# Sharing the sixteen transfers of a band between SyncE and GpSimd in another way

## The chip, the cores and the metric

The kernel runs on one core of one Trainium2 chip. The metric is the device time in microseconds of one execution; the time of a kernel is the median of its runs.

## What is computed

The input x holds 32 images of 256 channels and 32 x 32 pixels. Two layers follow each other, each with a group norm of its input (32 groups of 8 channels) in front and the input added behind:

```python
x = x + conv3x3(groupnorm(x))        # inputs and product rounded to 10 bits of mantissa, plus bias
x = x + involution7x7(groupnorm(x))
# the involution, n = groupnorm(x):
y = relu(batchnorm(w1 @ n))                     # 64 channels
w = (w2 @ y + b2).reshape(16 groups, 49 taps, 32, 32)
out[g, c] = sum over taps of w[g, tap] * patch of n[g, c] at tap      # 16 channels a group
```

So in the second layer every pixel has its own 7 x 7 filter for each of 16 groups, computed from the pixel itself.

## The kernel before

**Work and stages.** All 32 images pass through one pipeline that is written out by hand: a loop over slots `n` (line 537), sixteen to an image. In each slot it emits whatever is due in it. `front(b)` (line 275) is a generator that is advanced up to twice a slot and does the first layer of an image that comes later, up to the normed input `xn`, its reduced form `y_sb` and the transposed `pixels`. `sums(b, m)` (line 480) and `add_windows` (line 511) do the involution on PE and add its result to x.

**Bands.** The involution's sum over taps runs on PE as a product of pixels and of a band: for a piece of 8 rows of an image (`k`, four to an image, 128 in all) an SBUF tile of 128 pixels by 2 sides, in which the filters of each pixel stand at the place where they act. Three such tiles (`NBAND`, line 62) take turns. The filters have to be brought from one layout to another, and that is done through a scratch tensor `wd` in HBM:

- `weights(b, r0)` (line 390): PE computes the filters of four rows, DVE adds the bias and writes them to the ring `w_sb` (line 416).
- `scatter(b, k)` (line 454): seven transfers of 160 KB, from `w_sb` to `wd`, one for each column of the filter, all issued by SyncE (line 465).
- `load_bands(b, k)` (line 467): sixteen transfers (`JC`) of 70.2 KB, from `wd` to the band, each to eight partitions and two sides. With `SHARE = 8` SyncE (`nc.sync`) issues those with `i` 7 and 15, GpSimd (`nc.gpsimd`, the POOL of the profile) the other fourteen (lines 477 and 478).
- `sums(b, m)` reads the band on PE (line 503), two calls for each band; its first matmul waits for all sixteen transfers.

**Order around the change.** SyncE's queue carries everything else that moves: the loads of x (line 105, two of 512 KB for each image), the scatters, its two band transfers, and the stores of the result (line 524). GpSimd's queue carries, after its memsets at the start, band transfers alone. Each queue works in the order of the program. The scatter of band `k` of image `b` is emitted in slots 16b-13, 16b-9, 16b-5 and 16b-3 for k = 0 to 3, its loads in slot 16b+4k-9, its first sums in slot 16b+4k. Thus SyncE's band transfers stand behind the scatter of the next band in slots in which both are due, and ahead of those that follow. Completion is told by eight semaphores for SyncE's transfers and eight for GpSimd's, which are used in turn: a transfer isn't issued before the one eight earlier in its queue has landed. The first GpSimd transfer of a band also waits for the band's scatters and for PE's last use of the tile, and the first scatter that overwrites a part of `wd` waits for the loads that read it an image before.

Of the kernel before, what the change touches and what calls it, by code (L numbers as in the profile page):

```python
# [14 lines left out]
B, C, H, W = 32, 256, 32, 32  # L15
# [44 lines left out]
ROW = S * WPIX  # L60
WR = 4
NBAND = 3
SHARE = 8
NPIX = 6
RING = 24
FRONT = -56
# [5 lines left out]
def tile_quant_conv_then_involution(  # L72
# [16 lines left out]
    nc = tc.nc  # L89
# [377 lines left out]
    def load_bands(b, k):  # L467

        band = bands[(b * K + k) % NBAND]
        for i in range(JC):  # L470
            j = i // 2 + i % 2 * JC // 2
            src = bass.AP(
                tensor=wd.tensor,
                offset=wd.offset + k * TR * ROW + (j + PAD1) * WPIX,
                ap=[[ROW - 1, TR], [JC * WPIX, SIDES], [1, WPIX]],
            )
            queue = nc.sync if i % SHARE == SHARE - 1 else nc.gpsimd
            queue.dma_start(band[j::JC, :, j * WB : j * WB + WPIX], src)  # L478

    def windows(b, m):  # L480
# [49 lines left out]
    def due(n, lag):  # L530

        b, i = divmod(n - lag, per)
        return (b, i) if 0 <= b < B else (None, None)

    with tc.manual_schedule():
        fronts = {}
        for n in range(FRONT, B * per + 2):
            b, i = due(n, FRONT)
# [10 lines left out]
            b, i = due(n, 0)  # L549
            if b is not None and i % 2 == 0:  # L550
                sums(b, i // 2)
            b, i = due(n, 1)
# [6 lines left out]
            b, i = due(n, 2)  # L559
            if b is not None and i == 2 * (M - 1 - SIDES):  # L560
                store(b, 0)
            b, i = due(n, -LEAD)
# [3 lines left out]
            b, i = due(n, -LEAD + 1)  # L566
# [4 lines left out]
            b, i = due(n, LOAD)  # L571
# [3 lines left out]
            b, i = due(n, 3 - 4 * NBAND)  # L575
            if b is not None and i % 4 == 0:
                load_bands(b, i // 4)
# [37 lines left out]
```

## Time and profile before

| | us |
|---|---|
| median of three runs | 1411.43 |
| lowest and highest | 1402.78, 1411.64 |
| the profiled execution, its time | 1416.45 |
| its span, from the first to the last instruction | 1414.7 |
| GpSimd's first band transfer issued at | 77.3 |
| GpSimd's last band transfer issued at | 1401.3 |

The profile is of one execution. PE is TensorE's matmuls, PEld its loads of weights, DVE VectorE, ACT ScalarE, POOL GpSimd and SP SyncE, whose work is only to issue. In a line such as `POOL band L478 <- DMA band<-wd: 171.5, 223, 2.9` the engine and line that waited stand on the left, what ended the wait on the right, then the sum in us, the number of times and the longest. Where a page says `issue`, the profile shows nothing that was waited for. The granted TensorE clock is 0.978 of full speed over the span. By lines, the chain of work that ended last gives 24% of the span to band transfers, 19% to the convolution's matmuls, 15% to the involution's sums, 9% to the filters' matmuls, 7% to scatters and 5% to POOL's issuing of band transfers.

### The profile page before, as it was taken

What the parts mean: (1) busy time and instruction counts of PE and PEld (TensorE: products, weight loads), DVE (VectorE), ACT (ScalarE), POOL (GpSimd) and SP (SyncE); (2) the same over time, 40 slices, a digit from 0 to 9 for tenths busy, and PEclk for the clock granted to TensorE, in tenths of its full rate; (3) what the DMA queues carried; (4) which work ended last, traced back from release to release, by engine and by line L of the source; (5) the groups of instructions that cost most, each with busy time, mean ns of one, the idle gap of its engine ahead of it and who ended that gap; (6) DMA issues with size and microseconds to landing.
All of it is one profiled execution on the core that took longest, in us unless ns stands there. A gap on an engine that the chain in (4) does not pass through costs nothing.

```text
span 1414.7 us, 70076 instructions
## 1 busy us (share of the span) xinstructions
PE 1265.2 (89%) x29440; PEld 802.2 (57%) x29440; DVE 933.0 (66%) x3180; ACT 729.8 (52%) x1699; POOL 1003.5 (71%) x1817
## 2 busy tenths in 40 slices
PE   4899899999999899989999999999999999999665
PEld 1456565566565566655566556565566556655543
DVE  4567667767677677766767667767667676766642
ACT  5775555455555445555545555554556454553300
POOL 7067767686776777767777777677776767777774
PEclk9999999999999999999999999999999999999976
DMA  6099899999999999999999999999999999999995
GB/s 212 6 228 283 251 277 276 281 262 285 277 273 264 287 268 269 294 260 270 289 267 287 268 277 253 273 280 273 274 289 271 268 279 282 278 270 262 258 258 165
DMA packets 366232, 369.33 MB, mean 261 GB/s; under 512 B 78624, under 2 KB 308192, under 8 KB 365664
## 3 DMA queue, kind: packets, MB, share of 16 engines
q1 hardware_dynamic: 279904, 235.72, 57.2%
q0 software_dynamic: 86016, 129.14, 34.5%
q8 instruction: 234, 3.83, 1.2%
q14 instruction: 78, 0.64, 0.1%
HBM read 183.81 MB, written 180.74 MB: 258 GB/s over the span
## 4 chain that ended last, share of the span: by engine, by line
PE 47%; DMA 31%; issue 7%; POOL 5%; DVE 4%; ACT 3%; SPq 2%; POOLq 0%; DVEq 0%; ACTq 0%
DMA band<-wd 24%; PE pc L320 19%; PE acc L503 15%; PE pw L398 9%; DMA wd<-w_sb 7%; POOL band L478 5%; PE py L368 3%; DVE w_sb L416 2%; PE pt L383 2%; SPq L465 2%; ACT junk L210 1%; DVE x L519 0%; DVE w_sb L147 0%; ACT xn L269 0%; DVE q L334 0%
## 5 line engine op out<-in xcount | busy, mean ns | idle before, releaser
L478 POOL DMA_DIRECT2D band<-wd x1792 | 978.0, 548 | 397.8 <-DMA band<-wd 249.0
L416 DVE TENSOR_TENSOR w_sb<-pw,b_sb 128x16 f32<-128x16 f32 (+9 forms) x1920 | 454.0, 350 | 386.9 <-PE pw L398 363.2
L320 PE MATMUL pc<-xq,wq 128*128 128x496 f16 (+3 forms) x2304 | 536.5, 379 | 31.3 <-ACT xq L269 21.4
L503 PE MATMUL acc<-band,pixels 64*32 64x190 f32 (+1 forms) x16384 | 420.5, 323 | 78.9 <-DMA band<-wd 39.6
L503 PEld LDWEIGHTS acc<-band,pixels 64*32 64x32 f32 x16384 | 298.3, 108 | 171.1 <-issue 101.5
L320 PEld LDWEIGHTS <-wq 128*128 128x128 f16 x2304 | 206.4, 98 | 328.9 <-issue 114.6
L398 PE MATMUL pw<-w_sb,y 64*32 64x224 f32 (+1 forms) x8192 | 296.6, 333 | 31.1 <-issue 29.4
L519 DVE TENSOR_TENSOR x<-acc,x 128x380 f32<-128x380 f32 (+1 forms) x512 | 261.7, 511 | 35.7 <-PE acc L503 26.8
L398 PEld LDWEIGHTS pw<-w_sb,y 64*32 64x32 f32 x8192 | 182.8, 107 | 63.0 <-issue 43.9
L387 ACT COPY pixels<-pt 128x512 f32<-128x512 f32 x128 | 73.6, 575 | 238.2 <-PE pt L383 238.2
L210 ACT ACTIVATE junk<-x 128x512 f16<-128x512 f32 (+1 forms) x192 | 146.5, 763 | 20.7 <-DVE x L336 15.2
L210 ACT ACTIVATE junk<-x,mean 128x1024 f16<-128x1024 f32 x128 | 147.1, 1149 | 4.3
L241 ACT ACTIVATE s<-back,eps 128x2 f32<-128x2 f32 x64 | 18.9, 296 | 193.7 <-DVE back L226 193.6
L334 DVE TENSOR_SCALAR q<-pc 128x512 f16<-128x512 f32 x128 | 87.2, 682 | 16.5 <-PE pc L320 16.3
L269 ACT ACTIVATE xn<-x,off,rstd 128x512 f32<-128x512 f32 x128 | 96.1, 799 | 0.0
L336 DVE SCALAR_TENSOR_TENSOR x<-q,bias_sb,x 128x512 f32<-128x512 f16 x128 | 92.1, 719 | 0.2
L383 PEld LDWEIGHTS pt<-ident,xn 128*128 128x128 f32 x512 | 64.0, 142 | 27.4 <-issue 3.2
L383 PE MATMUL pt<-ident,xn 128*128 128x128 f32 x512 | 78.1, 275 | 0.9 <-ACT pixels L387 0.9
L231 ACT ACTIVATE mean<-back 128x2 f32<-128x2 f32 x64 | 12.7, 199 | 127.6 <-DVE back L226 127.6
L269 ACT ACTIVATE xq<-x,off,rstd 128x1024 f16<-128x1024 f32 x64 | 75.8, 1227 | 0.1
L368 PEld LDWEIGHTS py<-xn,w_sb 128*64 128x64 f32 x2048 | 63.0, 139 | 16.5 <-issue 8.1
L368 PE MATMUL py<-xn,w_sb 128*64 128x64 f32 x2048 | 67.8, 224 | 2.3 <-ACT xn L269 1.8
(40 smaller groups left out, 370.7 us busy)
## 6 DMA issues: line engine op xcount, KB each, us to landing
wd<-w_sb SPq DMA_DIRECT2D x896, 160.0 KB
band<-wd POOLq DMA_DIRECT2D x1792, 70.2 KB
x<-in_x SPq DMA_DIRECT2D x64, 512.0 KB
out<-x SPq DMA_DIRECT2D x64, 512.0 KB
band<-wd SPq DMA_DIRECT2D x256, 70.2 KB
band<-in_w SPq DMA_DIRECT2D x2, 1152.0 KB
w_sb<-in_w SPq DMA_DIRECT2D x2, 196.0 KB
wd<-band SPq DMA_DIRECT2D x2, 180.0 KB
```

Source lines behind the costliest of these rows:

```text
L210: nc.scalar.activation(junk[:, n0:n1], src[:, h, n0:n1], func, bias=bias, accum_out=self.sums[:, i : i + 1])
L269: nc.scalar.activation(dst, src, AF.Identity, bias=self.off[:, one], scale=self.rstd[:, one])
L320: nc.tensor.matmul(pc.rearrange("p (r c) -> p r c", c=W)[:, r0 - nt * RT : r1 - nt * RT, c0:c1], wq[:, kh, k, mh * P : (mh + 1) * P], xq[: ...
L334: nc.vector.tensor_scalar(q, pc, F16_MAX, -F16_MAX, ALU.min, ALU.max)
L336: nc.vector.scalar_tensor_tensor(xt[:, mh, cols], q, bias_sb[:, mh : mh + 1], xt[:, mh, cols], ALU.add, ALU.add)
L368: nc.tensor.matmul(py[i * CR : (i + 1) * CR, cols], w1_sb[:, kh, :], px[:, r : r + 2], start=kh == 0, stop=kh == CH - 1,)
L383: nc.tensor.transpose(pt[:, i, h * P : (h + 1) * P], xn[:, h, (m + i) * P : (m + i + 1) * P], ident)
L398: nc.tensor.matmul(pws[i][t * TW : (t + 1) * TW, r, : dj.stop - dj.start], y_sb[b % 2][half, (r0 // 2 + r) * W : (r0 // 2 + r + 1) * W], w ...
L416: nc.vector.tensor_tensor(to, pws[i][:p, r : r + rows, e, d0 * G : d1 * G].rearrange("p r (d g) -> p r d g", g=G), b2_sb[:p, e, d0 * G : d ...
L478: queue.dma_start(band[j::JC, :, j * WB : j * WB + WPIX], src)
L503: nc.tensor.matmul(at[t * TW : (t + 1) * TW, h, :, f - top : l - top], px[p, a, v * GC : v * GC + TW], of[:, :, 2 * a + v, f - top : l - top],
L519: nc.vector.tensor_tensor(x_at, of, x_at, ALU.add)
```

## The change

SyncE issues the last of the sixteen transfers of a band alone, and GpSimd fifteen. For the four bands of the last image SyncE issues every second one, eight, and GpSimd eight. Over the whole run SyncE has 156 band transfers where it had 256, and GpSimd 1892 where it had 1792. The transfers themselves, their order within a band and all other instructions stay as they are.

```diff
-SHARE = 8
+SHARE = 16
+LAST_SHARE = 2
...
     def load_bands(b, k):

         band = bands[(b * K + k) % NBAND]
+        share = LAST_SHARE if b == B - 1 else SHARE
         for i in range(JC):
             j = i // 2 + i % 2 * JC // 2
...
-            queue = nc.sync if i % SHARE == SHARE - 1 else nc.gpsimd
+            queue = nc.sync if i % share == share - 1 else nc.gpsimd
             queue.dma_start(band[j::JC, :, j * WB : j * WB + WPIX], src)
```

## The prediction

> **What bounds the kernel now.** I read the page first: busy times, then the DMA queues.
>
> ```profile
> PE 1265.2 (89%) x29440; PEld 802.2 (57%) x29440; DVE 933.0 (66%) x3180; ACT 729.8 (52%) x1699; POOL 1003.5 (71%) x1817
> ...
> q1 hardware_dynamic: 279904, 235.72, 57.2%
> q0 software_dynamic: 86016, 129.14, 34.5%
> ```
>
> No engine is full, but the two DMA queues (q1 is SyncE's, q0 is GpSimd's) together hold 91.7% of the sixteen DMA engines over the whole span, start and end included. So next I asked for the steady part in windows, restricted to what touches the bands. The columns are the stretch, its length, busy time and count of PE, PEld, DVE and POOL, the granted clock, the DMA share and GB/s.
>
> ```profile
> 100.00:400.00 300.00, 91.07 (x3648) 65.25 (x3648) 0.00 (x0) 220.63 (x405) 0.99 0.98 274
> 400.00:700.00 300.00, 93.88 (x3712) 66.84 (x3712) 0.00 (x0) 218.62 (x401) 0.99 0.97 275
> 700.00:1000.00 300.00, 90.16 (x3648) 64.26 (x3648) 0.00 (x0) 218.32 (x401) 1.00 0.98 273
> 1000.00:1150.00 150.00, 46.52 (x1856) 32.69 (x1856) 0.00 (x0) 113.46 (x209) 0.99 0.98 277
> ...
> 1210.00:1310.00 100.00, 32.23 (x1311) 22.50 (x1293) 0.00 (x0) 76.46 (x141) 1.00 0.96 272
> ```
>
> POOL's count is the number of band transfers that it issued: 1416 in 1050 us, one in 0.742 us, so a band of fourteen takes 10.38 us. The DMA engines stand at 0.978 there. The last line is a stretch in which nearly all loads of x are over (one pair is left, at 1228 us), and POOL goes at 0.709 us a transfer. Then I asked whom POOL waits for from 300 to 1200 us, and what its line looks like over the whole run (durations are min/median/max in ns):
>
> ```profile
> POOL band L478 <- DMA band<-wd: 171.5, 223, 2.9
> POOL band L478 <- issue: 38.6, 69, 5.9
> POOL band L478 <- DMA wd<-w_sb: 16.4, 27, 2.7
> POOL band L478 <- DMA x<-in_x: 3.8, 2, 3.0
> ```
>
> ```profile
> L478 POOL DMA_DIRECT2D band<-wd x1792: 547/547/683, 77.3 to 1401.3; - x200
> L478 SPq DMA_DIRECT2D band<-wd x256: 569/766/2121, 81.2 to 1388.6; - x128
> ```
>
> An issue takes POOL 547 ns. The rest of the 742 ns is mostly the first wait: each POOL transfer carries a wait for the one eight before it (eight completion semaphores in turn), so POOL has at most eight under way. By the trace's semaphore records the sixteenth increment comes 5.1 us after the issue on average, and eight issues last only 8 x 0.547 = 4.4 us. POOL hardly ever waits for PE to free a band, and little for scatters. So POOL runs without a pause that another engine imposes: it sets the pace, and what slows it is the time that its transfers spend in full DMA engines. PE is next: in the same windows without the restriction it is busy 280 of 300 us, 0.93, so a band can't get below some 9.7 us.
>
> **What the skill says.** "DMA: Bandwidth & Descriptors", section "Issuing engines are not separate DMA queues": transfers from all engines run on the same sixteen DMA engines. The trace agrees, since a transfer's descriptors are the same by both routes (16 of 4496 B, which took 253 ns each on average on both queues, by the packet records). By this the change takes no work from the DMA engines. Section "Why a DMA increments its semaphore by 16 and not by 1": the number of DMA engines for one transfer is the largest factor up to 16 of both outer dimensions; from SyncE the lowest-numbered are taken and the issuer adds the missing counts, from GpSimd consecutive ones from a moving start, and all sixteen count. A band transfer's outer dimension is 8. The trace agrees on the count: 249 of 256 transfers of SyncE show nine updates of their semaphore (eight engines, and one for the missing eight), POOL's show sixteen. Which eight they are, the trace doesn't tell; I take the page's word. Then SyncE's two transfers a band always go to the same eight DMA engines, two descriptors on each.
>
> **The change part by part.**
>
> (a) SyncE issues one transfer fewer for each of 124 bands: about 0.77 us of its queue (the median above). SyncE isn't the pace, so this is worth at most what others wait for scatters: POOL's 16.4 us in 900. I count nothing; the cover is SyncE's own waits for DVE. If the cover weren't there, 124 x 0.77 = 95 us would be at stake, but POOL's wait for scatters limits that to about 20 us.
>
> (b) POOL issues one more for each of these bands, 15 in place of 14. At the present pace it costs 0.742 us, at most 124 x 0.742 = +92 us. But the pace isn't fixed: it follows the load of the DMA engines. From the windows: DMA work per POOL transfer is 0.7415 x 0.9775 = 0.725 us in the steady part, and 0.709 x 0.96 = 0.681 us once the x loads are gone. Work fell by 0.044, the pace by 0.0325: 0.74 of each microsecond of DMA work shows in the time. The part that isn't DMA work is then 0.7415 - 0.74 x 0.725 = 0.21 us a transfer (0.14 to 0.28, since the shares have two digits). One transfer moved with total DMA work unchanged costs this part: +0.21 us a band, +26 us.
>
> (c) The eight DMA engines that SyncE's transfers use get relief. Per band they now have 14 (their part of POOL's) + 4 descriptors, the other eight 14. After the change it is 15 + 2 and 15. The fuller ones lose one descriptor, 0.253 us a band; the emptier ones gain one. POOL's next issue waits for all sixteen counts, so the fuller engines decide. At 0.74 this is worth 0.19 us a band, -23 us. From both sides: nothing if a transfer's slowest engine is as often one of the others, 0.253 us (-31 us) if the eight engines are the bound outright.
>
> (b) and (c) together: 124 x (0.21 - 0.19) = +2.5 us. For (c) I take the value at 0.74 and not zero, because 18 descriptors with the scatters and x come to more work than the others have, in engines that stand at 0.98 on average.
>
> (d) The last image: eight by SyncE and eight by POOL, where it was two and fourteen. Here is SyncE's end before:
>
> ```profile
> 1360.48 5.97 SPq L465 DMA_DIRECT2D wd<-w_sb  x7
> 1366.55 1.25 SPq L478 DMA_DIRECT2D band<-wd  x2
> 1368.17 5.62 SPq L465 DMA_DIRECT2D wd<-w_sb  x7
> 1373.89 1.54 SPq L478 DMA_DIRECT2D band<-wd  x2
> 1375.55 0.40 SPq L524 DMA_DIRECT2D out<-x  x1
> 1376.63 6.66 SPq L465 DMA_DIRECT2D wd<-w_sb  x7
> 1383.39 0.57 SPq L524 DMA_DIRECT2D out<-x  x1
> 1384.07 5.09 SPq L478 DMA_DIRECT2D band<-wd  x4
> ```
>
> POOL is relieved of 24 transfers, about 24 x 0.68 = 16 us (56 took from 1363.9 to 1401.85 us), and would be done long before. SyncE gets 24 more, at 0.57 to 0.77 us: 14 to 18 us. Twelve of them stand ahead of the last band's scatters, and the other twelve are behind everything, so nothing hides them, save some 2 us of SyncE's own waiting. Its last issue moves from 1389.2 to between 1401 and 1408 us; POOL's was at 1401.85. So SyncE takes over as the last, and the end moves by -1 to +6 us: I take +2.
>
> Sum: the profiled execution had a span of 1414.7 us in 1416.45 us. Its span becomes 1414.7 + 2.5 + 2 = 1419. That execution was 5 us over the median of 1411.43, so I forecast 1411.4 + 4.5 = 1416 us.
>
> **Rivals.** *POOL pays and nothing is given back.* The relief of eight engines doesn't show, because the counts of all sixteen come late alike. Then (b) stands alone, with its bounds: 124 x 0.14 to 0.28 = +17 to +35 us, plus the end: 1430 to 1448 us. At its far end, where the pace doesn't follow load at all, +92: 1505 us. For it: the waits of POOL are for its own transfers; POOL has no free time. Against: the pace did follow when the x loads stopped. *The eight engines are the bound outright.* Then a descriptor less is 0.253 us a band, and POOL's own part is hidden: -31 us, 1382 us; it decides as soon as POOL's waiting falls from 0.195 to below 0.144 us a transfer, because then 15 transfers take what 14 took (10.38/15 = 0.692). For it: engines at 0.98 on average with an uneven load; against: POOL's pace rose less than the work fell. PE's 0.93 leaves room for this gain, and for little more. *SyncE as the bound*, relieved by (a): at most 20 us, 1393 us; against it stands that it waits for DVE. *The change doesn't do what it says:* excluded; the program's order has 1892 transfers on POOL's queue and 156 on SyncE's, nothing else moved.
>
> **How the numbers follow.** A difference under 1% (14 us) is about what the measurement of this kernel can't tell from none: its three runs span 1402.8 to 1411.6. The forecast, that the two sides cancel, has 0.43, with its own range 1400 to 1425; POOL pays, 0.30 (of which 0.03 for over 1450); the eight engines or SyncE outright, 0.22, at 1382 to 1397; 0.05 for what I don't see, spread over both sides. That gives faster 0.25, same 0.43, slower 0.32. Leaving out some 0.1 at each end, the range is 1385 to 1450 us.
>
> **What would show it.** In the steady part POOL's count per 300 us should rise from 402 to about 430 (15 in 10.4 us), its mean spacing fall to 0.69 us, with less waiting for its own transfers, and the DMA share stay at 0.97 to 0.98. If POOL pays, the count stays near 415 and the DMA share falls to 0.95 or so. If the eight engines were the bound, the count is above 440. At the end SyncE's last band issue should come after POOL's. I'm wrong if PE begins to wait for bands more than the 12 us in 900 that it does now, or if scatters come late.

## The result, and the profile after

The changed kernel takes 1466.01 us (median of 4 runs, 1459.51 to 1472.25) where the one before took 1408.91 on the same chip (four runs, of which the forecast had three): a ratio of 1.041, with an interval of 1.036 to 1.045. The forecast was 1416 us with a range to 1450, so the time lies outside it, on the slow side. The two profiled executions differ a little less, 1462.67 us (span 1460.9) against 1416.45, because the one of before lay above its median and the one of after below.

The page of the changed kernel, its busy times and DMA queues:

```profile
PE 1264.7 (87%) x29440; PEld 811.0 (56%) x29440; DVE 932.5 (64%) x3180; ACT 729.6 (50%) x1699; POOL 1057.7 (72%) x1917
...
q1 hardware_dynamic: 277504, 228.52, 53.3%
q0 software_dynamic: 90816, 136.35, 35.0%
```

Only POOL works much longer than before, by 54 us: a hundred issues of 0.547 us. (The weight loads, PEld, have 9 us more; PE, VectorE and ScalarE have the same work.) 7.2 MB have gone over from q1 to q0, and the DMA engines are less full, 88.3% where they were 91.7%. The windows of the steady part, restricted to what touches the bands, with a stretch after the last load of x (issued at 1267.7 us):

```profile
100.00:400.00 300.00, 90.26 (x3584) 65.98 (x3584) 0.00 (x0) 226.89 (x417) 0.98 0.94 266
400.00:700.00 300.00, 88.89 (x3520) 64.18 (x3520) 0.00 (x0) 227.89 (x418) 0.99 0.94 266
700.00:1000.00 300.00, 89.63 (x3584) 63.94 (x3584) 0.00 (x0) 229.00 (x420) 0.99 0.93 263
1000.00:1150.00 150.00, 44.51 (x1728) 31.80 (x1728) 0.00 (x0) 107.56 (x198) 0.98 0.94 263
```

```profile
1280.00:1350.00 70.00, 22.36 (x896) 15.66 (x896) 0.00 (x0) 55.81 (x103) 1.00 0.93 261
```

POOL issued 1453 transfers in 1050 us, one in 0.723 us. It was one in 0.742: POOL got faster by 2.6%, where fifteen in place of fourteen needed 7%. So a band takes 15 x 0.723 = 10.84 us in place of 10.38. The DMA share fell to 0.94. These are the marks that the prediction had set for "POOL pays" (about 415 a stretch, 0.95), not for its own forecast (430, 0.97). POOL's waits from 300 to 1200 us, with PE's wait for bands under them (the last line is that of the kernel before), and POOL's and SyncE's lines over the whole run:

```profile
POOL band L480 <- DMA band<-wd: 137.3, 159, 3.4
POOL band L480 <- issue: 36.9, 46, 3.7
POOL band L480 <- DMA wd<-w_sb: 27.2, 33, 3.4
...
PE acc L505 <- DMA band<-wd: 47.0, 33, 3.3
...
PE acc L503 <- DMA band<-wd: 12.1, 8, 3.2
```

```profile
L480 POOL DMA_DIRECT2D band<-wd x1892: 547/547/681, 76.5 to 1443.7; - x190
L480 SPq DMA_DIRECT2D band<-wd x156: 567/602/1872, 80.7 to 1447.1; - x156
```

POOL waits less for its own transfers (137 us, it was 172), and SyncE issues its own faster (median 602 ns, it was 766). The relief is there, but it is small. Who waits now is PE: its wait for bands is 47.0 us where it was 12.1, which the prediction had named as a sign of being wrong. Its other sign, late scatters, shows faintly: POOL waits 27.2 us for them where it waited 16.4. They aren't the loss: in runs below with fifteen and with sixteen transfers on GpSimd that wait is 18.8 and 13.4 us. Of the end, SyncE's timeline:

```profile
1421.48 6.08 SPq L480 DMA_DIRECT2D band<-wd  x8
1427.66 0.40 SPq L526 DMA_DIRECT2D out<-x  x1
1428.41 6.37 SPq L466 DMA_DIRECT2D wd<-w_sb  x7
1434.88 2.44 SPq L526 DMA_DIRECT2D out<-x  x1
1437.42 10.27 SPq L480 DMA_DIRECT2D band<-wd  x16
```

SyncE issues the last band transfer, at 1447.1 us, after POOL's last at 1443.7. From POOL's last issue for the band before the last image to the end of the span it is 50.2 us; before it was 51.3. So the last image costs nothing, and the whole loss lies in the 124 bands before it: 48 us between the profiled executions, counted from POOL's first band transfer, and 57 between the medians, so 0.39 to 0.46 us a band.

### The profile page after: what moved, and what is told of

It reads as the page before. It is cut to its first block, busy times and chain, and to the rows that moved or that the text cites. A ratio compares the mean times of both kernels' runs of the same rounds, so it can differ in the third digit from the quotient of the medians.

```text
span 1460.9 us, 70087 instructions
## 1 busy us (share of the span) xinstructions
PE 1264.7 (87%) x29440; PEld 811.0 (56%) x29440; DVE 932.5 (64%) x3180; ACT 729.6 (50%) x1699; POOL 1057.7 (72%) x1917
## 4 chain that ended last, share of the span: by engine, by line
PE 42%; DMA 32%; DVE 7%; POOL 6%; issue 5%; SPq 5%; ACT 2%; POOLq 0%; DVEq 0%; ACTq 0%
DMA band<-wd 22%; PE pc L321 15%; PE acc L505 15%; DMA wd<-w_sb 9%; PE pw L399 9%; POOL band L480 6%; SPq L466 5%; DVE w_sb L417 4%; PE py L369 2%; PE pt L384 1%; DVE x L521 1%; ACT junk L211 1%; DMA out<-x 1%; DVE w_sb L148 0%; DVE q L335 0%
## 5 line engine op out<-in xcount | busy, mean ns | idle before, releaser
L480 POOL DMA_DIRECT2D band<-wd x1892 | 1032.2, 548 | 386.0 <-DMA band<-wd 221.3
L505 PEld LDWEIGHTS acc<-band,pixels 64*32 64x32 f32 x16384 | 303.2, 108 | 221.4 <-issue 128.1
L399 PE MATMUL pw<-w_sb,y 64*32 64x224 f32 (+1 forms) x8192 | 302.1, 337 | 22.0 <-issue 20.8
L399 PEld LDWEIGHTS pw<-w_sb,y 64*32 64x32 f32 x8192 | 189.4, 108 | 53.6 <-issue 38.6
```

The costliest lines, as they stand in the source:

```text
L399: nc.tensor.matmul(pws[i][t * TW : (t + 1) * TW, r, : dj.stop - dj.start], y_sb[b % 2][half, (r0 // 2 + r) * W : (r0 // 2 + r + 1) * W], w ...
L505: nc.tensor.matmul(at[t * TW : (t + 1) * TW, h, :, f - top : l - top], px[p, a, v * GC : v * GC + TW], of[:, :, 2 * a + v, f - top : l - top],
```

## Experiments

Times are medians, ratios are against the kernel before on the same chip, with a 95% interval; a gain or loss in us is the ratio's. A pace of POOL is always 1050 us, from 100 to 1150, over the band transfers counted there.

**The two halves of the change.** First the steady part alone, then the last image alone:

```diff
-LAST_SHARE = 2
+LAST_SHARE = 16
```

> The change without its last image: SyncE issues one of sixteen in all 128 bands. If GpSimd's fifteenth transfer is the whole loss (0.37 to 0.46 us a band), this is as slow as the changed kernel or a little slower, 1462 to 1475 us, since the last image then has fifteen on GpSimd as well. If the split of the last image were what cost time, this is well below the changed kernel, 1420 us or less.

1461.41 us, 1.041 (1.038 to 1.045): the whole loss.

```diff
-SHARE = 16
+SHARE = 8
 LAST_SHARE = 2
```

> The last image alone is changed: eight and eight there, two and fourteen elsewhere. The changed kernel's end, counted from the last issue of the band before the last image, is 50.2 us and before's 51.4, so the theory that GpSimd's count in the other images is the loss gives the time before, 1405 to 1412 us. The rival, that SyncE's late scatters at the end cost time, gives 1415 us or more.

1405.76 us, 1.002 (1.000 to 1.004): no difference that counts. What is left to explain is fifteen and one in place of fourteen and two.

**One transfer less, on either queue.** From the kernel before, a transfer of each band left out, SyncE's first (shown) or one of GpSimd's (`JC // 2 - 2` in the same place):

```diff
         for i in range(JC):
+            if i == JC // 2 - 1:
+                continue
```

> Leaves work out: of SyncE's two transfers of a band (fourteen stay on GpSimd) the first is not issued at all, so a column of the band keeps its old contents. It is the relief of SyncE and of its eight DMA engines without the transfer on GpSimd. The theory of the prediction (the eight engines decide, 0.74 of 0.253 us a band) gives -24 us or more, 1385 us or less. The theory that GpSimd's own queue sets the pace and hardly follows the DMA load gives at most a third of that, 1400 to 1410 us.

> Leaves work out: of GpSimd's fourteen transfers of a band one is not issued; SyncE keeps its two. The counterpart of the run without one of SyncE's. If a transfer on GpSimd costs three times one on SyncE, this gains 60 to 82 us, or less where PE, busy 0.93 of the time, stops it: 1325 to 1350 us. If both cost alike (data on the DMA engines alone), 24 us, about 1380 us.

Without SyncE's: 1378.09 us, 0.983 (0.979 to 0.987), a gain of 24 us. Without GpSimd's: 1380.64 us, 0.981 (0.976 to 0.986), 26 us. The first is what the prediction's relief had asked for. The second contradicts a simple price list, in which a transfer costs three times as much on GpSimd: at fourteen and two, taking a transfer from either queue is worth about the same. What the two runs share is a sixteenth of the band's data. But they don't end at the same limit. Here is one window without SyncE's transfer, then one without GpSimd's, and of the latter POOL's wait for scatters from 300 to 1200 us:

```profile
400.00:700.00 300.00, 93.84 (x3856) 67.53 (x3840) 0.00 (x0) 228.68 (x420) 1.00 0.96 277
...
400.00:700.00 300.00, 91.59 (x3704) 64.34 (x3688) 0.00 (x0) 210.92 (x386) 0.99 0.98 273
...
POOL band L480 <- DMA wd<-w_sb: 65.7, 30, 7.2
```

Without SyncE's transfer the DMA share falls to 0.96, and GpSimd's fourteen take 1050/1449 x 14 = 10.15 us a band (counts of 408, 420, 414 and 207). Without one of GpSimd's the share stays at 0.98, and POOL's wait for scatters goes from 16.4 to 65.7 us: it is GpSimd that waits there.

**The data, or the place in the queue.** A transfer of 1 KB in place of the real one: once added on GpSimd after the band's transfers (shown), once put where SyncE's was left out.

```diff
+    spare = const.tile([P, 2, 16], F32, name="spare")
+    few = bass.AP(tensor=w1.tensor, offset=w1.offset, ap=[[1000, TR], [64, SIDES], [1, 16]])
...
+        nc.gpsimd.dma_start(spare[:TR], few)
```

> The kernel before, with one more transfer on GpSimd for each band that moves 1 KB (sixteen pieces of 64 B into a spare tile) and nothing else: the issue and the completion semaphore of a fifteenth transfer without its data. From the runs so far a real transfer more on GpSimd costs the 58 us of the change and the 24 us that SyncE's relief gave, 82 us, and 0.6 us of other work there 30 us. If beside the issue the data counts alone, this costs about 30 us, 1430 to 1440 us. If the turn of the eight semaphores counts as well, 50 to 65 us, 1455 to 1468 us.

> Leaves work out: as in the run without SyncE's first transfer, but in its place SyncE issues one of 1 KB to a spare tile, so its queue is as long as before and only the data is gone. If it was the data on the DMA engines that gave 24 us, the gain stays: 15 to 25 us, 1378 to 1390 us. If it was SyncE's time or its semaphores, the gain is lost: 1398 to 1408 us.

On GpSimd the tiny transfer costs 65 us: 1471.52 us, 1.046 (1.039 to 1.053), at least as much as moving a real one there did (58), and a little over the range for the turn of the semaphores. So the loss of the change is not in the data of the fifteenth transfer; it is in its being there. On SyncE, with the data gone and the transfer still issued, 1393.60 us, 0.990 (0.981 to 0.998): 14 of the 24 us stay, within wide bounds. The run lies between the two expected ranges, nearer to the one of the data; how much SyncE's own issue is worth isn't settled by it.

**Other work in GpSimd's time.** The kernel before, with two fills of a small tile after each band's transfers:

```diff
+    spare = const.tile([P, BUSY], F32, name="spare")
...
+        for _ in range(2):
+            nc.gpsimd.memset(spare, 0.0)
```

> The kernel before, and after each band's transfers GpSimd also fills a small spare tile twice, about 0.6 us of its time for each band without any transfer. If GpSimd's own time sets the pace, each band is later by most of it: +50 to +75 us, 1460 to 1485 us. If the eight completion semaphores and the DMA engines set it, the work fits into time in which GpSimd waits anyway: +0 to +25 us, below 1435 us.

1433.22 us, 1.021 (1.018 to 1.024), +30 us. It fell between the two expectations. The fills, by the view of their tile:

```profile
L483 POOL MEMSET spare<- x256: 297/308/322, 85.8 to 1419.6; 128x240 f32 x128
```

0.62 us of POOL's time a band costs 0.23 us a band. A part of GpSimd's time was thus free in the kernel before: it isn't simply full. And the tiny transfer, at the same place and with 0.57 us of POOL's time, cost 0.51 us a band, over twice as much. So a transfer costs more on this queue than other work of the same length; whether that is the turn of the eight semaphores wasn't tried by itself.

**Whether the DMA engines still decide at fifteen.** GpSimd issues the first fifteen, the sixteenth is left out:

```diff
-            queue = nc.sync if i % SHARE == SHARE - 1 else nc.gpsimd
+            if i == JC - 1:
+                continue
+            queue = nc.gpsimd
```

> Leaves work out: GpSimd issues the first fifteen transfers of each band and nobody the sixteenth. It is the change in its other images with a sixteenth of the band's data taken off the DMA engines. At fourteen and two, taking a transfer's data away gave 24 to 26 us from either queue. If at fifteen GpSimd's turn of eight semaphores is the bound and no longer the DMA engines (a floor of 0.72 us a transfer, 10.8 us a band), it stays near the changed kernel: 1448 to 1466 us. If the DMA engines still decide, 1435 to 1443 us.

1467.15 us, 1.040 (1.036 to 1.045): as slow as the changed kernel, with a sixteenth less data. Its windows (counts 412, 417, 419 and 206 in the four stretches, two of them shown) have the pace of 0.722 us of the changed kernel:

```profile
400.00:700.00 300.00, 87.19 (x3524) 63.32 (x3526) 0.00 (x0) 227.74 (x417) 0.97 0.93 258
700.00:1000.00 300.00, 89.15 (x3568) 64.38 (x3573) 0.00 (x0) 228.51 (x419) 0.97 0.91 257
```

At fourteen leaving out SyncE's transfer was worth 24 us, at fifteen it is worth nothing, within some 8 us. This is the clearest sign that the bound has moved: from the DMA engines to GpSimd's queue.

**The transfer on a third queue.** SyncE one, ScalarE one, GpSimd fourteen; ScalarE's is issued three slots later (the last line):

```diff
+            queue = nc.sync if i == JC - 1 else nc.scalar if i == JC // 2 - 1 else nc.gpsimd
...
+            b, i = due(n, 6 - 4 * NBAND)
```

> SyncE issues one transfer of a band (i = 15), as after the change, but the other (i = 7) goes to ScalarE's queue and not to GpSimd's, and is issued three slots later there. GpSimd keeps fourteen. If the loss of the change is the fifteenth transfer in GpSimd's queue, this is about as fast as before, 1395 to 1415 us. If SyncE with one transfer less were the cause in any way (other order of its scatters or semaphores), it is as slow as the change, above 1440 us.

1414.70 us, 1.004 (1.001 to 1.007). SyncE with one transfer less costs 10 us at most here; the loss comes with the fifteenth on GpSimd.

**Whether eight DMA engines decide.** SyncE's first transfer of a band is replaced by a copy of the same number and size of pieces from x to HBM, once with outer dimension 8, once 16. The cut shows where the two runs differ:

```diff
-                of = bass.AP(tensor=x.tensor, offset=x.offset, ap=[[3 * 1200, TR], [1200, SIDES], [1, WPIX]])
-                nc.sync.dma_start(copied[:, :SIDES], of)
+                of = bass.AP(tensor=x.tensor, offset=x.offset, ap=[[1200, TR * SIDES], [1, WPIX]])
+                nc.sync.dma_start(copied, of)
```

> Leaves work out: SyncE's first transfer of a band is replaced by a copy of as many bytes in as many pieces (8 x 2 pieces of 4496 B) from x to a scratch tensor in HBM, outer dimension 8, so that it runs on eight DMA engines like the real one. Both theories: near the kernel before, 1395 to 1415 us; it is the other half of the next run.

> The same copy with outer dimension 16: sixteen pieces of 4496 B, one for each DMA engine. If the eight engines that SyncE's transfers use decide (the prediction's third part: 18 descriptors a band against 14), this takes one of the extra descriptors from them and is 20 us or more below the run with outer dimension 8. If only the mean load counts, the two are equal within 8 us.

1400.14 us and 1400.58 us: ratios of 0.993 (0.990 to 0.996) and 0.993 (0.991 to 0.995), and 1429 and 1428 transfers of POOL in 1050 us. The trace confirms what differs: 125 of 128 copies show nine updates of their semaphore in the first run, 126 show sixteen in the second. Spreading a transfer over twice the DMA engines makes no difference, within some 6 us. One thing stays open: both runs move as many bytes as the kernel before and are still 10 us faster than it. So of the 24 us that leaving out SyncE's transfer gained, up to 10 may lie in something other than its bytes, such as its wait for scatters or where it writes; no run tells.

**The other way.** SyncE three, GpSimd thirteen:

```diff
-SHARE = 8
+SHARE = 5
```

> The change the other way: SyncE issues three of sixteen transfers (i = 4, 9, 14), GpSimd thirteen, in all images. If GpSimd's queue is the loss and the two prices hold (82 us less, 24 us more), 1345 us or a little more where PE stops it, 1345 to 1375 us. If the eight DMA engines that SyncE's transfers use are by then the bound (13 + 6 descriptors a band against 13), it is no faster than before or slower, 1400 us or more.

1416.53 us, 1.007 (1.004 to 1.009). Slower as well, if only by 9 us, with the DMA share at 0.99 in three of four windows: nothing is to be had from GpSimd's queue when it isn't the bound. Why it isn't simply equal to before isn't settled; POOL's wait for scatters, which stand in SyncE's queue, is 34.2 us from 300 to 1200 us where it was 16.4. The time lies in the range of the eight DMA engines, but the two copies speak against that reason. Fourteen and two is the best of the splits that were run, and no run with all its work beats the kernel before.

**The price of a place, and what it depends on.** Sixteen on GpSimd; then the changed kernel with three of seven scatters left out after the first image:

```diff
-SHARE = 8
+SHARE = 32
```

> GpSimd issues all sixteen transfers of a band, SyncE none. If GpSimd's queue is the bound at a fixed 0.72 us a transfer, a band takes 16 x 0.72 = 11.5 us and the whole 1410 + 128 x (11.5 - 10.4) = 1551 us, within 1535 to 1565 us. If what SyncE has given up helps as it goes on (the elastic pace of the prediction), no more than another 58 us over the change: 1525 us or less.

```diff
+            if b > 0 and dj > 3:
+                continue
```

> Leaves work out: the changed kernel, with only the first four of seven scatters of a band after the first image, so three of seven filter columns are old ones, and some 3 x 16 pieces of 640 B a DMA engine and band are gone. GpSimd keeps fifteen transfers. If GpSimd's waits come from the landing time of its eight transfers under way, and that from the load of the DMA engines, its spacing falls from 0.72 towards 0.6 us and the time to where PE sets it, 1330 to 1390 us. If 0.72 us is a fixed price, it stays near the changed kernel, 1445 to 1466 us.

With sixteen: 1530.85 us, 1.089 (1.083 to 1.095), 4 us below the range that a fixed price gave and above that of the elastic one. Two of its windows, of which the first gives 300/425 = 0.706 us:

```profile
100.00:400.00 300.00, 87.45 (x3392) 62.94 (x3392) 0.00 (x0) 231.63 (x425) 0.97 0.90 253
400.00:700.00 300.00, 86.68 (x3328) 61.68 (x3328) 0.00 (x0) 228.12 (x419) 0.96 0.88 251
```

The counts of all four stretches are 425, 419, 425 and 211: 0.709 us a transfer, 11.35 us a band. But that average isn't what one place more costs. From fifteen in all bands (1.041) to sixteen (1.089) the time grows by 0.52 us a band (0.44 to 0.60): about the 0.547 us of an issue, and clearly less than 0.71. With four scatters the time is 1406.61 us, 1.002 (0.999 to 1.004), which neither expectation had:

```profile
400.00:700.00 300.00, 92.84 (x3776) 66.56 (x3776) 0.00 (x0) 239.97 (x440) 0.99 0.84 230
700.00:1000.00 300.00, 90.80 (x3712) 65.62 (x3712) 0.00 (x0) 236.33 (x434) 0.98 0.84 228
```

Counts of 428, 440, 434 and 214 make 0.693 us. So the pace isn't fixed: the spacing falls with the load of the DMA engines, but slowly, by 0.03 us while the share falls from 0.94 to 0.84. Over fifteen transfers a band that comes to 0.45 us, as much as the whole loss of the change; but it took 480 KB a band off the DMA engines, nearly seven transfers' worth, where at fourteen one was worth 24 us. The sixteenth increment of a transfer's semaphore, by the trace's records, comes 4.45 us after its issue there, 4.8 us in the changed kernel and 5.1 us before.

## Why the prediction was wrong

**What sets the pace** was half right. GpSimd's queue hardly ever stood still for another engine, and yet it wasn't the only bound. At fourteen and two the DMA engines, at 0.98, were the other: a transfer left out on either queue was worth 24 to 26 us. Without SyncE's transfer GpSimd's fourteen needed 10.15 us a band, with the DMA engines no longer full, so in the kernel before, at 10.38 us, what looked like a queue at its limit was in part one that followed. At fifteen that slack is used up: a transfer left out on SyncE gains nothing there.

How large the slack was isn't settled. At an average of 0.72 us a transfer, fourteen take 10.1 us, which leaves 0.3 us; then 0.62 us of fills should cost 0.3 us a band (0.23 measured), the fifteenth transfer 0.4 (0.39 to 0.46; the tiny one 0.51), and two more 1.1 (0.97). But the sixteenth transfer alone cost 0.52 and not 0.72, and with 0.52 for the fifteenth too the slack would be about 0.1 us, too little for the fills. So two bounds fit roughly, with no single price for a place and no single figure for the slack.

**Step (a)**, SyncE's queue is not the pace and counts for nothing: consistent with ScalarE's run. At most some 10 us, the difference of the two runs without SyncE's data, whose intervals overlap.

**Step (b) is the one that failed** first, and step (c) added to it. Of the 55 us between the sum of (b) and (c) and the measured loss, 31 are missing in (b) and 23 are the relief of (c), which didn't come. In (b): "The part that isn't DMA work is then 0.7415 - 0.74 x 0.725 = 0.21 us a transfer", hence +26 us. The slope of 0.74 came from two stretches of one profile, with and without the loads of x, and was taken for the answer of POOL's pace to DMA load of any kind. The changed kernel shows what was wrong. Its own stretch without loads of x has 103 transfers in 70 us, 0.680 us at a share of 0.93; with them it is 0.723 us at 0.94. At nearly the same share the pace differs by 0.04 us. By the trace it is the loads of x themselves, in bursts of two times 512 KB, that hold up POOL's transfers, and not the mean share. Here SyncE issues such a pair at 401.9 us; the lines are windows of 5 us around it:

```profile
396.90:401.90 5.00, 1.52 (x64) 1.15 (x64) 0.00 (x0) 3.79 (x7) 1.00 1.02 299
401.90:406.90 5.00, 1.52 (x64) 1.18 (x64) 0.00 (x0) 4.42 (x9) 1.00 0.89 257
406.90:411.90 5.00, 1.52 (x64) 1.12 (x64) 0.00 (x0) 2.07 (x4) 1.00 1.07 319
411.90:416.90 5.00, 1.52 (x64) 1.18 (x64) 0.00 (x0) 4.96 (x10) 1.00 0.91 247
```

(Windows this short count a packet where it starts, so a share can exceed 1.) Over all 24 pairs between 100 and 1150 us POOL issues one transfer in 1.18 us in the third of these windows and one in 0.69 us elsewhere, which is nearly the 0.68 of the stretch without loads. Scatters follow each pair, but scatters with no load of x ahead of them slow POOL to no more than 0.76 in the 12 us after them. No run took the loads out. For other load the pace hardly answers: 0.723 at 0.94 (the change), 0.722 at 0.92 (a sixteenth less data), 0.709 at 0.89 (sixteen on POOL), 0.693 at 0.84 (four scatters). At these shares GpSimd's transfers follow each other at about 0.7 us on average, nearly whatever they move. So the added transfer wasn't absorbed by an elastic pace: in place of 0.21 us a band it cost 0.39 to 0.46.

**Step (c)**, -23 us for the relief of eight DMA engines: it didn't come. The mechanism is refuted by the two copies, which differ in just that and take the same time, within some 6 us, where 20 or more had been expected; and a transfer less on GpSimd, which by the prediction's own account takes one descriptor from each of these engines where SyncE's takes two, gained as much. The trace had confirmed the count of eight; that the fuller eight decide was the prediction's inference and didn't hold. The 24 us that leaving out SyncE's transfer brought agreed with the step only in size: they come with a transfer taken away, and the change takes none away.

**Step (d)**, +2 us for the last image: right in that SyncE comes last there, and in size, between -1.1 us (spans) and +2.3 us (the run with the last image alone). POOL wasn't done "long before", though: its last transfer is issued 3.4 us ahead of SyncE's.

**The rivals.** "POOL pays" was the right mechanism, and its place and marks were right. Its size, +17 to +35 us, came from the same slope and was short; its far end of +92 us was too much, since some of GpSimd's time had been free. The range ended where that slope did, at 1450 us, and should have given more weight to a pace that doesn't follow.

## What to carry to other kernels

A queue that is never held up by another engine isn't proved to be the bound: its waits can come from a resource that is shared. Take work away from each side in turn, and see what each is worth and which side is full afterwards, before an added place in the queue is priced. An average spacing isn't the price of one place more. And a slope between two stretches of one profile holds only for the kind of load that differs between them.

## What the runs showed of the hardware that wasn't expected

A transfer of 1 KB on GpSimd's queue (570 ns of issue each) cost as much as moving one of 70 KB there from SyncE (65 and 58 us over the run), and over twice what fills of about the same time cost; with eight completion semaphores in turn the queue came to about one transfer in 0.72 us, of which 0.547 us is issue, while the DMA engines stood at 0.92 to 0.94. What makes up the other 0.17 us is only in part known: the waits for own transfers are most of it in the profile, and a load lower by 0.10 of the DMA engines took 0.03 us off. More semaphores, so more transfers under way, weren't tried.
